# Two layers of a decoder on one core: in the first feed-forward, the last four tiles leave the transform earlier

## The chip, the cores and the metric

The kernel runs on one core of one Trainium2 chip. The metric is the device time of one execution in microseconds (us); the numbers of before are the median of three runs, and one further execution was taken with the hardware profiler. Five engines work side by side in a core: TensorE (PE in the profile, its weight loads PEld) multiplies matrices into PSUM, VectorE (DVE), ScalarE (ACT) and GpSimd (POOL) work elementwise, and SyncE (SP) here only issues transfers (DMAs).

## The reference, cut to what matters

The program is a decoder of two layers on `x` of 4 batches x 512 tokens x 512 features, each with self-attention, cross-attention and a feed-forward, every one followed by a residual sum and a layer norm. The change lies in the feed-forward of the first layer:

```python
gate = bitlinear(x, w_gate)                     # x in 8 bits per token, weights in {-1, 0, 1}
up = bitlinear(x, w_up)                         # both 512 -> 2048
intermediate = jax.nn.silu(gate) * up
return h_bitlinear(intermediate, w_down)        # act_quant(fwht(intermediate)) @ ternary(w_down).T
```

`fwht` is a Walsh-Hadamard transform over the 2048 features of a token. `act_quant` needs the largest value of a token after the transform, so nothing behind the transform can start for a token before all its 2048 features are there.

## The kernel before, in words

**Phases and lanes.** The six sublayers are phases A to F (C is the feed-forward of the first layer, D the self-attention of the second), and each phase is done for the batches 0 to 3: `ORDER` lists A0 ... F3. Each such task is a Python generator that emits some work and yields. `lanes` keeps two tasks alive and lets each emit one step in turn; I call one such turn a round. A new task starts when fewer than two are alive and the youngest one has yielded "next". So C1 runs beside C0, and is 16 rounds behind it; C2 starts in the round after C0 ends, C3 16 rounds behind C2, and D0 when C2 ends. Beside the lanes some weight preparation is advanced by one step per round (`BESIDE`): while C3 and D0 run, it loads and splits the weights of D.

**What sets the order.** The order of emission is a priority, not the final order: the tile framework places every instruction on its engine's queue by its own estimate of when operands and buffers are ready, and takes the earlier emitted one of those that are ready. On the chip each engine then works through its queue in order.

**Delays inside a task.** `Pipe.later(n, fn)` puts a piece of work on a list, and `tick()`, called at the start of each step, runs what has come due after `n` steps; `drain()` makes steps until the list is empty.

**Phase C of one batch (`l0_ffn`).** The 2048 features are 16 tiles of 128, tokens along the free axis (512). A step `o` of the loop at L734 multiplies gate and up of one tile (`pg` L740 and `pu` L742, 4 matmuls each, bf16). One step later `gate` multiplies by the token's scale (DVE, L709) and applies silu (ACT, L710). Two steps after that, `up` multiplies by the up part (DVE, L714) and splits the product into a rounded part `hh` (ACT, L716) and a rest `hl` (POOL, L717). Two steps later `had` multiplies both by the 128 x 128 Hadamard matrix (`ph`, two matmuls, L722 and L723: the transform's two passes). One step later `keep` copies `ph` from PSUM to `hw` (ACT, L728), and two steps after the copy SP stores `hw` to a scratch array in DRAM (L731). So tile 15, multiplied in step 15, is transformed in step 20, copied in step 21 and stored in step 23, and `drain` makes 8 steps after the loop.

The other half of the transform mixes the 16 tiles with one another. For that the scratch array is read back as 16 tiles `z` of 128 tokens' rows (SP, L253; the call stands behind the drain), with the 2048 features of a token rearranged; because every `z` tile holds rows from all 16 stores, the loads wait for the landing of the last store. Two more steps pass, and then 16 steps `had2` (L808, four matmuls in groups recorded as eight on the page) finish the transform. Behind each four of these come the largest value per token (DVE, L754), a copy (`q2f`, ACT, L756), the quantization (ACT L774, DVE L775), transposes (`q2T`, PE L781, copied by ACT at L786), and the down projection `dn` (16 matmuls, PE, L794).

Tiles of one kind share buffers: `g`, `hh`, `hl`, `hw` and others of a task take turns in 13 slots (`T_BUFS`), larger-lived ones such as `z`, `q2f` and the weights in 69 (`O_BUFS`), and all PSUM tiles in 8 banks.

Of the kernel before, what the change touches and what calls it, by code (L numbers as in the profile page):

```python
# [23 lines left out]
NT = 4  # L24
# [44 lines left out]
class Net:  # L69
# [590 lines left out]
    def l0_ffn(self, b):  # L660
        nc = self.nc
        pipe = Pipe()
# [50 lines left out]
        def up(o, pu, g):  # L713
            nc.vector.tensor_tensor(g, pu, g, ALU.mult)  # L714
            hi, lo = self.t("hh", F32R), self.t("hl", F32R)
            nc.scalar.copy(hi, g)  # L716
            nc.gpsimd.tensor_tensor(lo, g, hi.bitcast(F32), ALU.subtract)  # L717
            pipe.later(2, had, o, hi, lo)

        def had(o, hi, lo):  # L720
            ph = self.pb("ph")
            nc.tensor.matmul(ph, self.had, hi, start=True, stop=False)  # L722
            nc.tensor.matmul(ph, self.had, lo, start=False, stop=True)  # L723
            pipe.later(1, keep, o, ph)

        def keep(o, ph):
            w = self.t("hw")
            nc.scalar.copy(w, ph)  # L728

            to = scratch[:, o * P : (o + 1) * P, :].rearrange("i p t -> p i t")  # L730
            pipe.later(2, lambda: nc.sync.dma_start(to, w.rearrange("p (i t) -> p i t", i=NT)))  # L731

        tern = self.tern
        for o in range(16):  # L734
# [688 lines left out]
```

## Time and profile before

| | |
|---|---|
| time before, median of 3 runs | 1580.09 us (1579.72 to 1582.03) |
| the profiled execution's own time | 1580.57 us |
| its span, first to last instruction | 1578.9 us (1.67 us lie around it) |
| mean granted TensorE clock in it | 0.994 |
| PE busy in the span | 1512.4 us (96%) |
| DVE, ACT, POOL busy | 1214.0 us, 1041.7 us, 687.8 us |
| phase C, first gate matmul of C0 to last `dn` of C3 | 456 us to 759 us |

Durations further on come from the one profiled execution, and times of day are us from the start of its span. In the waits view a row names who waited for whom, with the total, how often, and the longest. In the timeline a row has the start, the length from the first to the last of a group, the engine, the line, the operation, the tiles (out<-in), the count, and in brackets how long the engine was idle before it and what ended that. In the table by stretches an engine's busy time is followed by its number of instructions, and PEclk is the share of the full clock that the throttle granted to TensorE.

### The profile page before, as it was taken

How to read it: one execution, taken by the hardware profiler on the slowest of the kernel's cores; microseconds unless marked ns; L12 is line 12 of the kernel's file. 1: busy time of each engine (PE TensorE's matmuls, PEld its weight loads, DVE VectorE, ACT ScalarE, POOL GpSimd, SP SyncE). 2: the span in 40 equal slices, each digit the busy share in tenths (PEclk: the TensorE clock that was granted, in tenths of full speed). 3: DMA queues.
4: the chain of work that ended last, by engine and by line, in shares of the span. 5: the costliest groups of instructions: out<-in, count | busy, mean ns of one | idle time of the engine just before them, and what ended most of it. 6: DMA issues, size and time to landing. Idle time of an engine off the chain costs nothing.

```text
span 1578.9 us, 25669 instructions
## 1 busy us (share of the span) xinstructions
PE 1512.4 (96%) x8222; PEld 1090.9 (69%) x8222; DVE 1214.0 (77%) x2594; ACT 1041.7 (66%) x2240; POOL 687.8 (44%) x704
## 2 busy tenths in 40 slices
PE   8999998999999999999999999999999999999996
PEld 6888775555544764477777668777687677787885
DVE  6486688898876678777577797767886898888896
ACT  5334667888778877887696864969634445545554
POOL 6665783656535303430435323353324344344342
PEclk9999999999999999999999999999999999999998
DMA  7044874444224534753434345633336630020101
GB/s 256 29 160 140 266 235 151 156 165 139 71 74 126 189 132 131 208 180 130 134 101 120 103 140 148 173 96 91 130 119 220 233 113 12 20 81 1 54 1 54
DMA packets 138759, 200.72 MB, mean 127 GB/s; under 512 B 17776, under 2 KB 52592, under 8 KB 138624
## 3 DMA queue, kind: packets, MB, share of 16 engines
q1 hardware_dynamic: 127584, 178.03, 35.5%
q10 hardware_dynamic: 6912, 12.59, 2.8%
q0 software_dynamic: 4128, 8.46, 2.2%
q8 instruction: 65, 1.06, 0.3%
q14 instruction: 70, 0.57, 0.1%
HBM read 121.94 MB, written 51.90 MB: 110 GB/s over the span
## 4 chain that ended last, share of the span: by engine, by line
PE 50%; DVE 11%; ACT 9%; issue 6%; DMA 3%; POOL 2%; SPq 0%; ACTq 0%; DVEq 0%; POOLq 0%
PE fg L1238 7%; PE facc L1221 5%; DVE fg L1194 3%; PE dT L986 3%; PE dn L794 2%; PE bo L500 2%; PE pg L740 2%; ACT de L976 2%; PE pu L742 2%; PE do L1006 2%; PE bT L249 2%; PE had L808 2%; PE bs L528 2%; PE ds L961 2%; PE dq L155 1%
## 5 line engine op out<-in xcount | busy, mean ns | idle before, releaser
L1194 DVE SCALAR_TENSOR_TENSOR fg<-fg,gs,fg 128x512 f32<-128x512 f32 x220 | 163.1, 745 | 30.4 <-ACT fg L1186 15.6
L976 ACT ACTIVATE de<-de,dm 128x128 f32<-128x128 f32 (+3 forms) x256 | 142.8, 562 | 11.5 <-DVE dm L972 11.3
L1238 PE MATMUL fg<-fxh,gu 128*128 128x512 f32 x352 | 140.4, 399 | 6.2 <-DVE fg L1194 3.1
L972 DVE CUSTOM_DVE_ANT_0 de<-ds,negm,thr 128x128 f32<-128x128 f32 (+3 forms) x256 | 126.3, 546 | 18.4 <-PE ds L961 15.8
L1238 PE MATMUL fg<-fxl,gu 128*128 128x512 f32 x352 | 137.5, 391 | 0.1
L717 POOL TENSOR_TENSOR hl<-g,hh 128x512 fp32r<-128x512 f32 x64 | 83.2, 1307 | 110.8 <-ACT hh L716 90.7
L484 POOL TENSOR_SCALAR be<-be,bsm 128x512 f32<-128x512 f32 x128 | 93.4, 742 | 85.3 <-DVE bsm L482 53.7
L1198 POOL TENSOR_TENSOR fg<-fg,fg 128x512 f32<-128x512 f32 x44 | 60.1, 1367 | 140.3 <-DVE fg L1194 56.7
L478 ACT ACTIVATE be<-bs,bsm 128x512 f32<-128x512 f32 x128 | 87.3, 689 | 32.4 <-DVE bsm L476 31.0
L898 POOL TENSOR_TENSOR dql<-dqf,dqh 128x512 fp32r<-128x512 f32 x32 | 41.4, 1295 | 150.6 <-ACT dqh L897 150.5
L986 PE MATMUL dT<-ident,de 128*128 128x128 f32 x640 | 91.3, 278 | 8.4 <-ACT de L976 6.4
L986 PEld LDWEIGHTS dT<-ident,de 128*128 128x128 f32 x640 | 71.7, 141 | 27.5 <-ACT de L976 14.8
L1238 PEld LDWEIGHTS fg<-fxh,gu 128*128 128x128 f32 x352 | 66.0, 188 | 30.6 <-DVE fg L1194 13.5
L476 DVE TENSOR_REDUCE bsm<-bs 128x1 f32<-128x512 f32 x128 | 83.0, 674 | 2.3 <-PE bs L528 2.3
L249 PEld LDWEIGHTS bT<-ident,be 128*128 128x128 f32 x512 | 54.9, 141 | 29.5 <-issue 15.6
L1238 PEld LDWEIGHTS fg<-fxl,gu 128*128 128x128 f32 x352 | 66.2, 188 | 12.8 <-DVE fxl L147 0.4
L1186 ACT ACTIVATE fg<-fg,gs 128x512 f32<-128x512 f32 x88 | 60.1, 683 | 20.6 <-PE fg L1238 20.6
L249 PE MATMUL bT<-ident,be 128*128 128x128 f32 x512 | 71.2, 280 | 1.4 <-POOL be L484 0.9
L500 PE MATMUL bo<-bpT,cT 128*64 128x512 f32 x256 | 71.4, 618 | 1.0 <-ACT bpT L491 1.0
L1212 POOL TENSOR_TENSOR fhl<-fg,fhh 128x512 fp32r<-128x512 f32 x44 | 58.5, 1330 | 29.9 <-ACT fhh L1211 29.7
L740 PE MATMUL pg<-qT,tb 128*128 128x512 bf16 x256 | 66.8, 381 | 4.4 <-ACT qT L702 2.8
L1190 ACT ACTIVATE fg<-fg,gs 128x512 f32<-128x512 f32 x44 | 30.3, 689 | 60.5 <-PE fg L1238 60.4
(357 smaller groups left out, 4685.3 us busy)
## 6 DMA issues: line engine op xcount, KB each, us to landing
x<-x SPq DMA_DIRECT2D x176, 256.0 KB, 3.2
had_scratch<-hw SPq DMA_DIRECT2D x64, 256.0 KB, 2.3
z<-had_scratch SPq DMA_DIRECT2D x64, 256.0 KB, 5.9
stk<-dqh SPq DMA_DIRECT2D x192, 64.0 KB, 2.1
tw<-in_wd_t SPq DMA_DIRECT2D x32, 256.0 KB, 4.0
p<-in_gu_p SPq DMA_DIRECT2D x22, 256.0 KB, 3.1
gu_codes<-gu SPq DMA_DIRECT2D x22, 256.0 KB, 3.1
gu<-gu_codes SPq DMA_DIRECT2D x22, 256.0 KB, 4.6
```

The lines of the kernel that those rows point to most:

```text
L249: self.nc.tensor.transpose(pt[:, i * P : (i + 1) * P], srcs[i][:, j * P : (j + 1) * P], self.ident)
L476: nc.vector.tensor_reduce(sm[:, h : h + 1], ps, AX.X, ALU.max, negate=True)
L478: nc.scalar.activation(e, ps, AF.Exp, bias=sm[:, h : h + 1], accum_out=sm[:, 2 + h : 3 + h])
L484: nc.gpsimd.tensor_scalar(es[h][i], es[h][i], sm[:, 4 + h : 5 + h], 1.0, ALU.mult, ALU.mult)
L500: nc.tensor.matmul(po[0][h * 64 : h * 64 + 64, :], cT[j][:, c : c + 64], pTs[h], start=j == 0, stop=j == NT - 1)
L717: nc.gpsimd.tensor_tensor(lo, g, hi.bitcast(F32), ALU.subtract)
L740: nc.tensor.matmul(pg, tern["wg_t"][k, c][:, m], qT[k], start=k == 0, stop=k == NT - 1)
L972: nc.vector.tensor_tensor_reduce(es[i], ps, self.negm[:, 384 - P * i :], -1.0, self.thr[:, i : i + 1], ALU.add, ALU.min, n4[:, i : i + 1])
L976: nc.scalar.activation(es[i], es[i], AF.Exp, bias=n4[:, i : i + 1], scale=-1.0, accum_out=den[:, hh * 4 + i : hh * 4 + i + 1])
L986: nc.tensor.transpose(pt[:, o + (i - j) * P : o + (i - j + 1) * P], es[i][:, j * P : (j + 1) * P], self.ident)
L1194: self.emitted["DVE"] = nc.vector.scalar_tensor_tensor(y[u], ps, s, y[u], ALU.mult, ALU.add)
L1238: nc.tensor.matmul(ps, self.gu[i, u][:, g * P : (g + 1) * P], xT[g][n], start=n == 0, stop=n == 1)
```

## The change

For the tiles `o` of 12 and over, `had` calls `keep` at once where it had put it off by one step, and `keep` puts the store off by one step where it had been two. For the tiles under 12 nothing changes. No instruction is added or removed; the last tile's store is emitted two steps earlier, so that the drain behind the loop of gate tiles has 6 steps where it had 8, in each of the four batches.

```diff
             nc.tensor.matmul(ph, self.had, lo, start=False, stop=True)
-            pipe.later(1, keep, o, ph)
+
+            if o < 12:
+                pipe.later(1, keep, o, ph)
+            else:
+                keep(o, ph)
 
         def keep(o, ph):
             w = self.t("hw")
             nc.scalar.copy(w, ph)
 
             to = scratch[:, o * P : (o + 1) * P, :].rearrange("i p t -> p i t")
-            pipe.later(2, lambda: nc.sync.dma_start(to, w.rearrange("p (i t) -> p i t", i=NT)))
+            pipe.later(2 if o < 12 else 1, lambda: nc.sync.dma_start(to, w.rearrange("p (i t) -> p i t", i=NT)))
```

## The prediction

> **What bounds the kernel now.** I read the page first: whom the time belongs to.
>
> ```profile
> PE 1512.4 (96%) x8222; PEld 1090.9 (69%) x8222; DVE 1214.0 (77%) x2594; ACT 1041.7 (66%) x2240; POOL 687.8 (44%) x704
> ...
> PE 50%; DVE 11%; ACT 9%; issue 6%; DMA 3%; POOL 2%; SPq 0%; ACTq 0%; DVEq 0%; POOLq 0%
> ```
>
> TensorE is busy in 96% of the span. The change adds no PE work and takes none away, so all it can move is PE's idle time, 66.5 us in the whole span, and the clock at which PE runs. Next, the waits of PE in the stretch of phase C (440 to 770 us):
>
> ```profile
> PE had L808 <- DMA z<-had_scratch: 3.4, 2, 2.4
> PE pg L740 <- ACT qT L702: 2.8, 2, 1.9
> ...
> ```
>
> The first row is the one that the change aims at: twice, 3.4 us in all, the second half of the transform waits for `z`, which waits for the last store. It can only be at the ends of C1 and C3: behind C0 and C2 the gate matmuls of the next batch fill PE. I look at the end of C1, PE first (two answers of the timeline):
>
> ```profile
> 543.12 0.48 PE L722 MATMUL ph<-hh,had 128*128 128x512 f32 x1
> 543.44 0.40 PE L723 MATMUL ph<-hl,had 128*128 128x512 f32 x1
> ...
> 555.14 1.13 PE L808 MATMUL had<-had,z 128*128 128x128 f32 x8 [2.38 <-DMA z<-had_scratch]
> ```
>
> The last tile's passes end at 543.84, and PE stands for 2.38 us until 555.14. What lies between is on ACT and SP:
>
> ```profile
> 543.37 1.09 ACT L786 COPY q2T<-q2T 128x1024 bf16<-128x1024 bf16 x1
> 544.27 1.40 ACT L774 ACTIVATE q2f<-q2f,am 128x512 f32<-128x512 f32 x2
> 545.51 0.64 ACT L756 COPY q2f<-had 128x512 f32<-128x512 f32 x1
> 545.97 0.66 ACT L728 COPY hw<-ph 128x512 f32<-128x512 f32 x1
> 546.45 1.42 ACT L774 ACTIVATE q2f<-q2f,am 128x512 f32<-128x512 f32 x2
> 547.69 0.65 ACT L756 COPY q2f<-had 128x512 f32<-128x512 f32 x1
> 548.15 0.68 ACT L728 COPY hw<-ph 128x512 f32<-128x512 f32 x1
> ...
> ```
>
> ```profile
> 548.85 0.36 SPq L731 DMA_DIRECT2D had_scratch<-hw  x1
> 551.24 1.76 SPq L253 DMA_DIRECT2D z<-had_scratch  x4
> ```
>
> The copy of tile 15 could have started at 543.84 and starts at 548.15: 4.31 us behind work of C0 that stands ahead of it in ACT's queue (tile 14: 3.49 us). SP doesn't hold anything up: the store goes out at the end of the copy, lands 2.27 us later, the first `z` goes out 0.12 us after that and takes 3.76 us. Last, what the standstill does to the clock, in the table by stretches (PEclk is the third figure from the right):
>
> ```profile
> 494.00:498.00 4.00, 2.14 (x11) 0.98 (x9) 2.41 (x4) 3.23 (x6) 1.35 (x2) 1.00 0.23 66
> 552.70:555.10 2.40, 0.05 (x1) 0.00 (x0) 2.40 (x6) 1.96 (x3) 0.00 (x0) 1.00 0.94 265
> 556.40:559.80 3.40, 3.40 (x10) 1.20 (x9) 1.36 (x3) 2.71 (x5) 0.00 (x0) 0.50 0.97 299
> 559.80:563.00 3.20, 3.20 (x31) 2.36 (x30) 1.44 (x3) 1.01 (x1) 0.00 (x0) 1.00 1.04 386
> ```
>
> From 556.4 to 559.8 the granted clock is half. The down projection of those us takes 5.30 us for its 16 matmuls, where those of 565.81 and 574.34 take 3.62: 1.68 us more. So this one wait costs 2.38 + 1.68 = 4.06 us.
>
> **The change part by part.** *The copy at once (16 copies: four tiles, four batches).* ACT does the same copies, 0.57 to 0.70 us each, only ahead of a round's other work. At the end of C1 the copy of tile 15 finds ACT in the `q2T` copy that ends at 544.46, and tile 14's may come between, until 545.1. It thus starts 0 to 1.3 us after its passes; I take 0.6 and a gain of 3.7 us (bounds 3.0 and 4.3). At the end of C3 the passes end at 698.61 and the copy starts at 701.56, 2.95 us late; with the same 0.6 the gain is 2.3. Should a copy reach the head of ACT's queue before its passes are done, ACT waits in order, with silu, the `hh` casts and `q2f` queued behind it, and POOL, DVE and then PE behind those. The row nearest to that is ACT waiting for `ph` before `hw`: 1.1 us in two waits over the 64 copies. Sixteen such waits of 0.4 to 0.6 us would be 6 to 9 us of ACT, which is idle for 2 to 6 us in every 20 us of the gate steps, so in part on the path; nearest is that row of 1.1 us, in which no wait of PE lies. I take 0.
>
> *The store after one step.* SP's queue carries the same 64 stores of 0.36 us each. They pass no transfer of this batch, since `z` needs all of them. In C2 they and `z` are moved past the last loads of D's weights (SP issues those from 640 to 654 us, between the stores); the weights are needed at 672 us by the `bo` matmuls, and SP issues one in 0.46 us, so a delay of one or two of them is hidden. I take 0; uncovered it would be the 0.4 us of the wait that the `bo` matmuls show. The `hw` buffers come free a step sooner; ACT waits for buffers of this pool in hardly any place (0.7 us for a landing store), worth -0.7 to 0, taken as 0.
>
> *The drain, two steps shorter.* This moves more than it seems. All of C0 behind its drain is emitted two rounds earlier against C1's gate steps, C1's own end two rounds earlier as well, and C2 starts two rounds sooner; C2 and C3 repeat it, and from D0 on all is as it was, four rounds sooner. Three places count.
>
> (a) End of C1. Chain before, from the end of the passes to `had2`: 555.14 - 543.84 = 11.30 us; PE's cover, work of C0, lasted until 552.75, 8.91 us. The chain falls by 3.7 to 7.6 us. The cover changes too: there are two rounds of C0 less in it. Two `had2` groups (2 x 0.9) and the first down projection (3.45) now come before C1's last passes, 5.3 us; the second down projection (3.45) and its neighbours' transposes (two, 0.9 in all) come into reach, 4.4 us, if ACT has delivered them. ACT is full here, 18.88 of the 20 us from 530 to 550, but only 13.95 of the 20 before, where two rounds of C0 now move, so I think it will. Cover 8.0 us, chain 7.6: the wait closes, narrowly. Gain 2.38, and with it the slow clock, 1.68.
>
> (b) End of C3: chain 708.50 - 698.61 = 9.89, wait 0.97, cover 8.92. After: chain 7.6, cover 8.0. Gain 0.97.
>
> (c) C0 and C2: `had2` comes two gate steps earlier. In C0 it started at 517.24; a gate step is 2.2 us, so it would stand at 512.8. The first `z` landed at 512.67, and this can't be earlier, as C0's last copy followed its passes at once (504.63 to 504.67). That just fits. Cost 0 to 2.2 us (one gate step), taken as 0.3, near the row. In C2, 668.37 less two steps of 2.45 is 663.5; `z` went out at 661.41 and landed at 665.99, but its copy was 3.2 us late, which goes. Cost 0 to 2.5 us, taken as 0.2.
>
> Sum against the profiled execution: 2.38 + 1.68 + 0.97 - 0.5 = 4.5 us off its own time of 1580.57 (span 1578.9 and 1.67 around it), 1576.1. The median of the runs stands 0.48 lower, so that I predict 1575.6. What is late next is ACT's `q2T` copy before a down projection (1.4 us of PE's waits now).
>
> The row says that a wait of 2.38 us was followed by half clock, while the 1.86 us from 494.46 and the 0.97 us from 707.53 were not. [...]
>
> **The rivals.** *The cover goes with the chain (slower).* Place: the ends of C1 and C3. If the second down projection isn't ready there, the cover is 8.91 - 5.3 = 3.6 us in both against a chain of 7.6: two waits of 4.0 us. Each is followed by a slow stretch of 1.7 us. Together 11.4 against 5.0 now, 6.4 us more: about 1586.5. It decides from the point at which the two waits with their clocks exceed 5.0 us, that is from some 1 to 2 us of wait in each place. For it: that projection's last operand came at 554.17, 10 us behind the passes. Against it: ACT has room in the rounds before.
>
> *A draw.* Chain and cover shrink alike; C1's wait stays near 2 us with its slow clock, C3's goes: 1579. For it: both are a matter of two rounds.
>
> *It doesn't do what it says.* The copies' priority rises by one round only; ACT's queue is arranged by estimated readiness, and a copy that the estimate takes to be ready late stays behind C0's work; then the chain and the wait remain: 1580. For it: tile 14's copy, due a round earlier than tile 15's, was as late. Against it: in C0 copies do start 0.04 us after the passes.
>
> **How the numbers follow.** The forecast gets 0.50, with a range of its own of 1573.5 to 1576.9; slower 0.23; the draw 0.15; nothing 0.12. About 0.2% or 3.2 us is what a measurement of this kernel can tell from no change. So faster 0.50, same 0.27, slower 0.23. The range goes from 1573.0 (all of the 5.0 us, and 2 us of small waits behind) up to 1584.5, which takes in the draw, nothing, and the lighter half of the slower rival.
>
> **What would show it.** Right: PE's wait for `z` under 1 us in all; tile 15's copies at the ends of C1 and C3 within 1.3 us of their passes; no half clock between 540 and 720 us; the last `dn` of C3, at 759 us before, some 4 us sooner, and the rest of the program shifted by that. Wrong: a wait for `z` of 2 us or more, at whichever batch; a second slow stretch; or a gain in phase C that is given back in phase D or F, where PE's queue would then be in another order.

## The result, and the profile after

The changed kernel is slower: 1591.57 us, the median of four runs (1586.68 to 1593.28), against 1580.95 us (1579.72 to 1582.03) for the kernel before. The ratio is 1.0065, with a 95% interval of 1.0043 to 1.0087. The same kernel run once more on another chip, against the kernel before on that chip, gave 1.0081 (1.0067 to 1.0094).

The page of the changed kernel, the rows that answer to those shown of before:

```profile
PE 1517.7 (95%) x8222; PEld 1092.4 (69%) x8222; DVE 1215.9 (76%) x2594; ACT 1041.8 (65%) x2240; POOL 687.8 (43%) x704
PE 47%; DVE 13%; ACT 9%; issue 6%; DMA 4%; POOL 2%; SPq 0%; ACTq 0%; DVEq 0%; POOLq 0%
```

The profiled execution is the slowest of the four (1593.28 us). Its span is 1591.6 us against 1578.9 before, 12.7 more. PE has as many instructions as before, but is busy for 5.3 us more (1517.7 against 1512.4) and idle for 7.4 us more (73.9 against 66.5). So there are two things to find: new waits, and the same matmuls at a lower clock. The waits of PE in phase C (440 to 790 us), who waited for whom, total, how often, longest:

```profile
PE had L812 <- DMA z<-had_scratch: 4.6, 1, 4.6
PE had L812 <- DVE q L779: 3.4, 1, 3.4
PE pg L744 <- ACT qT L702: 2.8, 2, 1.9
...
PE ph L723 <- POOL hl L717: 1.2, 2, 0.9
...
PE had L812 <- ACT hw L732: 0.7, 1, 0.7
```

The wait for `z` that the change aimed at is there in both places and longer: 3.42 us at the end of C1 (2.38 before) and 4.57 us at the end of C3 (0.97 before). The second row names DVE, but this is the same wait: the first `z` landed at 557.88 us and DVE's `q` ended within 0.01 us of it. The last two rows have no like before: 1.2 us for `hl` (0.88 in C1 and 0.36 in C3), and 0.7 us for `hw` at a `had2` of C2. Here is the end of C1 on PE:

```profile
545.57 0.50 PE L723 MATMUL ph<-hl,had 128*128 128x512 f32 x1 [0.88 <-POOL hl L717]
545.91 3.63 PE L798 MATMUL dn<-tb,q2T 128*128 128x512 bf16 x16
...
551.00 0.40 PE L723 MATMUL ph<-hl,had 128*128 128x512 f32 x1
551.24 0.62 PE L785 MATMUL q2T<-ident,q 128*128 128x128 bf16 x8
551.70 2.90 PE L812 MATMUL had<-had,z 128*128 128x128 f32 x24
558.02 1.13 PE L812 MATMUL had<-had,z 128*128 128x128 f32 x8 [3.42 <-DVE q L779]
558.98 5.30 PE L798 MATMUL dn<-tb,q2T 128*128 128x512 bf16 x16
```

The last tile's passes end at 551.40, 7.56 us later than before, because C0's first down projection (545.91) and one more `had2` group now run ahead of them. Only 3.20 us of C0's work lie behind the passes (until 554.60), where there were 8.91. Then PE stands until C1's first `had2`, and the down projection behind that takes 5.30 us where the one ahead took 3.63: the clock again. ACT and SP in the same stretch (timeline):

```profile
543.49 0.65 ACT L716 CAST hh<-g 128x512 fp32r<-128x512 f32 x1
545.44 0.68 ACT L716 CAST hh<-g 128x512 fp32r<-128x512 f32 x1
551.56 0.57 ACT L732 COPY hw<-ph 128x512 f32<-128x512 f32 x1
552.50 1.03 ACT L790 COPY q2T<-q2T 128x1024 bf16<-128x1024 bf16 x1
```

```profile
552.16 0.36 SPq L735 DMA_DIRECT2D had_scratch<-hw  x1
554.54 1.75 SPq L253 DMA_DIRECT2D z<-had_scratch  x4
```

The change does what it says: the copy starts 0.16 us behind the passes (4.31 before), the store goes out at once, and the chain from the passes to `had2` falls from 11.30 to 6.62 us. The first two rows show another side of it. The `hh` casts of the tiles 14 and 15 come at 543.49 and 545.44, where they came at 537.01 and 539.56: C0's quantization, moved two rounds earlier, and copies of earlier tiles stand ahead of them on ACT. Which of the two makes PE wait for `hl`, the first two experiments tell.

The clock, in the table by stretches (PEclk is the third figure from the right):

```profile
554.60:558.00 3.40, 0.00 (x0) 0.01 (x1) 2.26 (x8) 1.48 (x4) 0.28 (x1) 1.00 0.65 178
559.10:562.40 3.30, 3.30 (x10) 1.15 (x8) 0.69 (x1) 0.58 (x1) 0.00 (x0) 0.50 0.95 289
716.10:722.80 6.70, 5.45 (x17) 3.17 (x18) 1.12 (x2) 1.66 (x4) 0.00 (x0) 0.50 0.94 289
1142.80:1146.10 3.30, 3.30 (x8) 1.31 (x9) 1.88 (x5) 1.47 (x5) 1.75 (x3) 0.50 0.59 222
```

Half clock follows both waits. The stretch at 559 had its like before (556.4). New are the one behind the wait of C3, 6.83 us long, in which PE was busy for 5.45 us (its `dn` matmuls there start 427 ns apart, against 216 ns at the full clock, so that I put the loss at half of this, 2.7 us), and one at 1142.7 (1.7 us lost). These two make 4.4 of the 5.3 us of additional busy time; the other 0.9 us I can't put to a place. That the stretch at 1142.7 is the change's doing isn't shown: the second profile of the changed kernel has none there but one at 938.2, and the faster kernel of the first experiment has one at 927.4. Of the 7.4 us of additional idle time 7.0 lie in phase C.

By stage, PE is 0.6 us late at the first gate matmul of C0 already (458.56 us against 457.97; the 456 us in the table of before is the start of the transposes ahead of it), 2.9 us at the start of C2 (behind the end of C1), 3.8 us at C2's last gate steps, and 11.6 us at the end of C3. This stays so through phase D, and the stretch at 1142.7 adds most of the rest. So phase C carries 11.0 us of the 12.7, and no later stage gave more than 1 us back.

### The profile page after: what moved, and what is told of

Same layout as the page of the kernel before. It is cut to its first block, busy times and chain, and to the rows that moved or that the text cites. A ratio compares the mean times of both kernels' runs of the same rounds, so it can differ in the third digit from the quotient of the medians.

```text
span 1591.6 us, 25678 instructions
## 1 busy us (share of the span) xinstructions
PE 1517.7 (95%) x8222; PEld 1092.4 (69%) x8222; DVE 1215.9 (76%) x2594; ACT 1041.8 (65%) x2240; POOL 687.8 (43%) x704
## 4 chain that ended last, share of the span: by engine, by line
PE 47%; DVE 13%; ACT 9%; issue 6%; DMA 4%; POOL 2%; SPq 0%; ACTq 0%; DVEq 0%; POOLq 0%
PE fg L1242 7%; PE facc L1225 5%; PE dT L990 3%; PE dn L798 3%; DVE fg L1198 3%; ACT de L980 2%; PE bo L500 2%; PE had L812 2%; PE do L1010 2%; PE bT L249 2%; PE pu L746 2%; PE pg L744 2%; PE ds L965 1%; PE dq L155 1%; PE bs L528 1%
## 5 line engine op out<-in xcount | busy, mean ns | idle before, releaser
L812 PE MATMUL had<-had,z 128*128 128x128 f32 x512 | 67.2, 281 | 8.7 <-DMA z<-had_scratch 4.6
L1190 ACT ACTIVATE fg<-fg,gs 128x512 f32<-128x512 f32 x88 | 60.1, 683 | 20.8 <-PE fg L1242 20.6
L812 PEld LDWEIGHTS had<-had,z 128*128 128x128 f32 x512 | 63.0, 194 | 12.2 <-DVE q L779 8.3
```

Of the source, the lines that this page charges most:

```text
L812: nc.tensor.matmul(ps[:, c * P : (c + 1) * P], z[i * 4 + g][:, c * P : (c + 1) * P], self.had16, start=True, stop=True)
```

## The experiments

Each kernel was timed against the kernel before on its own chip; there the kernel before had medians from 1577.35 to 1578.22 us, so ratios are compared, not times. The first two experiments are to tell two theories apart: that the waits come from the lost cover (C0's rounds shifted against C1's), or from the copies and stores in their new places.

**The changed kernel with its two rounds given back**, ahead of the loads of `z`:

```diff
         yield from pipe.drain()
 
+        yield
+        yield
         z = [self.load(self.o("z"), ...
```

> The changed kernel with two empty steps put back between the drain and the z loads, so that only the early copy and store are left of the change and the lanes stand to each other as before. Theory (the shorter drain took PE's cover away at the ends of C1 and C3): PE's queue there is that of before, 8.9 us of C0's (C2's) work between the last passes and the first second-transform group, and the chain falls from 11.3 and 9.9 us to some 7 to 8; no wait for z at either place, no half clock there, so 1580.9 less 3 to 5 us: 1576 to 1578. Rival (the copies at once and the early stores disturb ACT's and SP's queues): it stays slow, 1588 to 1593.

Measured: 1575.62 us, ratio 0.9989 (0.9979 to 0.9998). PE's order is that of before again, and the wait for `z` is nearly gone:

```profile
PE had L814 <- DMA z<-had_scratch: 0.6, 1, 0.6
```

The early copies and stores alone lose nothing on balance. The gain over the kernel before is 1.7 us on the medians, less than the theory's 3 to 5. The trace shows why in part (rows of PE and ACT at the end of C1, then of PE at the end of C3):

```profile
542.87 0.45 PE L723 MATMUL ph<-hl,had 128*128 128x512 f32 x1
545.74 0.67 ACT L732 COPY hw<-ph 128x512 f32<-128x512 f32 x1
...
692.10 0.50 PE L723 MATMUL ph<-hl,had 128*128 128x512 f32 x1 [0.85 <-POOL hl L717]
694.08 0.50 PE L723 MATMUL ph<-hl,had 128*128 128x512 f32 x1 [0.36 <-POOL hl L717]
```

The last passes of C1 end at 543.33 here, near their old time, and the copy of tile 15 starts 2.41 us behind them, not 0.16 us; the first `z` lands 8.55 us behind the passes, 0.2 us before C1's first `had2`, so that the wait closes narrowly. And PE waits 1.2 us for `hl`, as long as in the changed kernel, though no round is shifted.

**The kernel before with the drain alone shorter**; copies and stores as before:

```diff
         ln = self.ln_tile()
-        yield
-        yield
```

> The kernel before, with copies and stores as they were, but without the two steps between the z loads and the second transform, so that C0's work behind its drain is two rounds earlier against C1's gates, as in the changed kernel. Theory: the cover falls to some 3 to 4 us as in the changed kernel while the chain isn't shortened, so waits for z of 6 to 8 us at the ends of C1 and C3 with a slow clock behind each: slower than the changed kernel or like it, 1591 to 1600. Rival (copies and stores are to blame): as before, 1579 to 1583.

Measured: 1595.66 us, ratio 1.0116 (1.0103 to 1.0129). PE at the ends of C1 and C3 (rows of the timeline):

```profile
549.06 0.40 PE L723 MATMUL ph<-hl,had 128*128 128x512 f32 x1
...
558.78 2.05 PE L806 MATMUL had<-had,z 128*128 128x128 f32 x8 [6.13 <-DMA z<-had_scratch]
...
720.88 2.05 PE L806 MATMUL had<-had,z 128*128 128x128 f32 x8 [4.67 <-DMA z<-had_scratch]
```

The passes end at 549.46, the cover is 3.19 us, the same as in the changed kernel, and without the shorter chain the wait is 6.13 us. So the two rounds cause the loss, and the early copies and stores win part of it back. That refutes the rival. PE waits for no `hl` here, so that this wait comes from the early copies and not from the two rounds alone: all profiles that have it have the copies at once. A third wait for `z` is at C2's `had2`, 2.53 us, where the first experiment had 0.6 and the changed kernel none.

**The order on PE.** In the instruction order of both kernels, C1's first `had2` group stands ahead of C0's second down projection. If that order is what takes the cover away, one more step ahead of `had2` in C1 and C3, which puts the down projection first, closes the wait in either kernel:

```diff
         yield
         yield
+        if b % 2:
+            yield
         q2T = {}
```

In the kernel before:

> The kernel before with one more empty step ahead of the second transform in C1 and C3 alone; in PE's queue the second down projection of C0 (C2) then stands ahead of the first second-transform group of C1 (C3), where before it stood behind it. Theory with the queue's order as the reason of the waits: 3.45 us more cover against unchanged chains of 11.3 and 9.9 us, so no wait for z at the end of C1 (2.4 before) nor of C3 (1.0), no half clock there: 1580.9 less 3 to 5, 1576 to 1578. Rival (the down projection isn't ready in time, ACT is what is short): PE waits for ACT's q2T copy instead, 1579 to 1583.

Measured: 1580.03 us, ratio 1.0018 (1.0009 to 1.0027). The timeline of PE at the end of C1 has no gap now:

```profile
542.34 3.62 PE L796 MATMUL dn<-tb,q2T 128*128 128x512 bf16 x16
...
550.37 3.72 PE L796 MATMUL dn<-tb,q2T 128*128 128x512 bf16 x16
```

The second down projection starts at 550.37 instead of 556.10. But the kernel didn't get faster. Its waits of PE in phase C:

```profile
PE pg L740 <- ACT qT L702: 4.9, 3, 2.2
PE dn L796 <- ACT q2T L788: 2.2, 2, 1.7
PE had L810 <- DMA z<-had_scratch: 1.2, 1, 1.2
```

One of C1's last down projections now waits 1.67 us for `q2T` (589 us), and C3's first gate matmul waits 2.15 us for `qT` (until 642.3) with half clock behind it until 645.7; C2's `had2` waits 1.2 us. The theory was right on the place and wrong on the total, which lies in the rival's range; the rival's wait for `q2T` is there too, but not where it was expected.

In the changed kernel:

> The changed kernel with the same one more step in C1 and C3. Theory: cover 3.2 plus 3.45 us against chains of 6.6 and 7.8 us, so waits for z of 0 to 1.2 us where the changed kernel has 3.4 and 4.5, and mostly no slow clock: 7 to 10 us off its 1591.6, 1581 to 1585. Rival (ACT is short, the down projection isn't ready): 1588 to 1593.

Measured: 1583.76 us, ratio 1.0041 (1.0026 to 1.0057): as expected. No wait for `z` is left at the end of C1 and 1.0 us at that of C3, and the same wait of 2.1 us for `qT` appears, with half clock from 642.8.

**The rounds given back at another place**: four steps instead of two behind the loads of `z` in the changed kernel, so that `z` goes out two rounds before it would with the first experiment's edit:

```diff
         ln = self.ln_tile()
         yield
         yield
+        yield
+        yield
```

> The changed kernel with two more empty steps behind the z loads instead of ahead of them: the loads are emitted as early as in the changed kernel, the second transform as late as in the kernel before. Theory (cover): PE's queue and the chain are those of the padded drain (e1), SP issues z when the last store has landed in both: the same time as e1 within 2 us, 0.997 to 1.001 of the kernel before, no wait for z at the ends of C1 and C3. Rival (z emitted early gets in the way of other transfers on SP): 1.005 or more.

Measured: 1574.92 us, ratio 0.9980 (0.9969 to 0.9991). PE waits for no `z` in phase C, and for no `hl`. This version is faster than both kernels, by 2.9 us on the medians against the kernel before.

**The two halves of the change.** Copy at once, store two steps later as before (the drain has 7 steps): only the `if o < 12` of `had` is kept.

> Half of the change: for the last four tiles the copy at once, but the store two steps behind it as before; the drain has 7 steps. In PE's queue the first down projection of C0 then still stands behind C1's last passes, as before the change, and only one second-transform group (0.9 us) has moved ahead of them: cover 8.0 us against a chain of 7 to 8. Theory (cover and chain, decided by where that projection stands): no wait for z or one under 1 us at the ends of C1 and C3, 0.997 to 1.001 of the kernel before. Rival (each step off the drain costs alike, half of the changed kernel's loss): 1.003.

Measured: 1581.74 us, ratio 1.0031 (1.0019 to 1.0042). Store one step after the copy, copy one step after the passes (7 steps as well): only the `2 if o < 12 else 1` of `keep` is kept.

> The other half: the copy one step behind the passes as before, the store one step behind the copy; the drain has 7 steps too. PE's queue is that of e6. Theory: cover 8.0 us, and a chain that is as long as before where the copy waits in ACT's queue (11.3 and 9.9 us): waits for z of about 3.3 and 1.9 us, mostly with a slow clock behind them, 1.001 to 1.004 of the kernel before, and slower than e6 by 3 us or more. Rival (the shorter drain alone counts, the copy's place doesn't): the same time as e6 within 1.5 us.

Measured: 1583.78 us, ratio 1.0041 (1.0027 to 1.0056), 2.0 us more than the copy's half: between the theory's 3 us or more and the rival's 1.5 or less. C1's first `had2` in the one and in the other (timeline of PE):

```profile
554.28 1.13 PE L811 MATMUL had<-had,z 128*128 128x128 f32 x8 [0.90 <-DMA z<-had_scratch]
```

```profile
554.39 1.13 PE L808 MATMUL had<-had,z 128*128 128x128 f32 x8 [2.72 <-DMA z<-had_scratch]
```

The waits at the ends are near the theory's: under 1 us in the first, and 2.72 and 1.26 us in the second, where it had about 3.3 and 1.9. The time of the first isn't, it is the rival's: its waits at the ends are under 1 us and no half clock lies in phase C, yet it is 3.9 us slower on the medians. PE is idle for 14.7 us from 440 to 780 us, where it was for 11.9 in the profile of before and 13.4 in a second one. The second is the one to compare with, since it lacks 31 matmul records as this one does, and a missing record counts as idle time. Against it I can place a wait of C2's `had2` for `z` (1.26 us) and three waits for `hl` (1.2 us), less 0.9 us that the waits at the ends of C1 and C3 are shorter. The rest of the 3.9 us stays open.

**The copy's half with its round given back**: that kernel and one `yield` ahead of the loads of `z`.

> The copy-only half (e6) with one empty step put back ahead of the z loads, so that the lanes stand to each other as before and only the place of the 16 copies is changed. Theory (the shift of the lanes costs, the copies don't): 0.997 to 1.000 of the kernel before, some 0.3 to 0.5% under e6. Rival (e6's 1.0031 came from the copies' new place in ACT's queue): 1.002 to 1.004, like e6.

Measured: 1575.53 us, ratio 0.9989 (0.9979 to 1.0000). The copies in their new place cost no more than they win (PE waits 1.2 us for `hl` here too); the loss of the half is that of its one round.

**One round less and nothing else**: the kernel before without one of its two steps behind the loads of `z`.

> The kernel before with one of the two empty steps behind the z loads taken out: half of e3's shift, copies and stores as before. PE's queue at the end of C1 is that of e6 and e7, the first down projection of C0 still behind C1's last passes. Theory: cover 8.0 us against chains of 11.3 and 9.9: waits for z of about 3 and 2 us, like e7, 1.003 to 1.005, less than half of e3's 1.0116, since the down projection hasn't changed its place. Rival (every step costs the same): 1.0055 to 1.0065.

Measured: 1587.73 us, ratio 1.0070 (1.0055 to 1.0085), above the theory and nearer to the rival. At the end of C1:

```profile
556.89 2.04 PE L807 MATMUL had<-had,z 128*128 128x128 f32 x8 [4.22 <-DMA z<-had_scratch]
```

The cover was 8.04 us, as expected of one round. The chain was what I had wrong: the copy started 4.9 us behind the passes (4.31 before), which makes it 12.26 us. Half clock for 6.83 us followed here, and 3.41 us at C3.

**Does it repeat?** The changed kernel, unaltered, on another chip:

> The changed kernel, unaltered, timed again beside the kernel before on one chip, since its ratio rests on four runs. Theory: the waits for z at the ends of C1 and C3 are there again, 3 to 4.5 us each, the last passes of C1 again some 5 to 8 us later than in the kernel before, and the ratio lies within 1.005 to 1.009; with e3 at 1.0116 and e1 at 0.9989 the early copies and stores are then worth some 0.3 to 0.6% inside the shortened drain. Rival (a good part of the 1.0065 was the slow clock of single executions): 1.003 or less.

Measured: 1589.89 us, ratio 1.0081 (1.0067 to 1.0094). Its waits for `z` are 3.16 us at C1, with no half clock behind it, and 3.31 us at C3, with half clock. A further profile of the kernel before:

> The kernel before, unaltered, one more profile, to see which of its own numbers belong to the execution and which to the kernel. Theory: the wait for z at the end of C1 is there again (1.5 to 2.5 us) and about 1 us at the end of C3; whether the clock halves behind the first depends on where the wait falls in the windows in which the clock is set (the starts of half clock within each trace lie whole multiples of 3.413 us apart), so it may be missing, and the time is then 1.7 us shorter. Rival: the half clock stands behind that wait in every execution.

Measured: 1579.98 us in that one execution. The wait at C1 is 2.25 us, and half clock follows at 556.7; at C3 it is 0.49 us. So these two profiles agree with the rival as well; it is the two of the changed kernel that differ, with half clock behind the wait at C1 in one of them only.

The experiments in one table. All times are us in the profiled execution: the chain from the end of the last passes to the first `had2`, the cover that PE has behind those passes, and the wait, first for C1 and then for C3.

| kernel | steps less | chain / cover / wait, C1 | chain / cover / wait, C3 | ratio |
|---|---|---|---|---|
| before | 0 | 11.30 / 8.91 / 2.38 | 9.89 / 8.92 / 0.97 | 1 |
| copy only | 1 | 8.93 / 8.04 / 0.90 | 8.96 / 8.04 / 0.92 | 1.0031 |
| store only | 1 | 10.76 / 8.04 / 2.72 | 9.30 / 8.04 / 1.26 | 1.0041 |
| one step less | 1 | 12.26 / 8.04 / 4.22 | 11.29 / 8.05 / 3.24 | 1.0070 |
| changed | 2 | 6.62 / 3.20 / 3.42 | 7.76 / 3.19 / 4.57 | 1.0065 |
| two steps less | 2 | 9.32 / 3.19 / 6.13 | 7.86 / 3.19 / 4.67 | 1.0116 |

The cover depends only on how many rounds C0 is shifted, not on what shortened the drain. One round costs 0.9 us, a `had2` group that goes in front. The second costs 4.85 us: the first down projection (3.45), a group's transposes and one more `had2` group go in front of the last passes, and nothing follows at the other end. The times don't follow the cover alone: the first round taken out of the kernel before cost 0.70%, the second some 0.46% more.

**What stays open.** Where the rest of the loss lies in the kernels that are one round shorter, and why the down projection put first gives its gain back at C1's last down projections and C3's first gate step, is seen only as waits for `qT`, `q2T` and C2's `z`; no experiment separates them. A version that keeps C0's work early and puts the last passes ahead of the first down projection wasn't tried.

## Why the prediction was wrong

**The copy, the store (right in the changed kernel, with luck).** I put the copy 0.6 us behind its passes; it came 0.16 us behind at both ends. But that was behind passes that themselves came 7.56 us later at C1. In the setting that I had in mind, with the passes near their old time, the copies came 2.41 and 2.42 us behind them (the first experiment), still behind C0's work on ACT, and the gain of 3.7 us at C1 would have been 1.9. The store followed, and SP held nothing up. The chain was predicted at 7.6 us and was 6.62 and 7.76; the difference between the two lies in the landing of the store, 2.26 us after its issue at C1 and 3.54 at C3. The copies were not free, though. I had written that casts queue behind a copy on ACT and that POOL and PE then wait, and had taken it as 0; PE's waits for `hl` came to 1.2 us in both profiles of the changed kernel and in that of the first experiment. It is less than the copies win: the ratio with the rounds given back was 0.9989.

**The cover (the step that failed).** Part (a) took 5.3 us out of the cover and put 4.4 back: "the second down projection ... come into reach, ... if ACT has delivered them", and so "Cover 8.0 us"; part (b) took the same 8.0 for C3. It was 3.20 and 3.19. The 5.3 us went as worked out (8.91 - 3.20 = 5.7), the 4.4 never came. ACT had delivered: the `q2T` copy for that projection ended at 553.53 us, and the projection ran at 558.98. It stood behind C1's `had2` in PE's queue, and PE took the two in that order (558.02, then 558.98), so it waited for a `z` that it doesn't need. The trace of before shows the same order (ACT, then PE):

```profile
553.15 1.02 ACT L786 COPY q2T<-q2T 128x1024 bf16<-128x1024 bf16 x1
...
555.14 1.13 PE L808 MATMUL had<-had,z 128*128 128x128 f32 x8 [2.38 <-DMA z<-had_scratch]
556.10 5.30 PE L794 MATMUL dn<-tb,q2T 128*128 128x512 bf16 x16
```

The operand was there at 554.17, and PE stood idle until 555.14 with a ready down projection in its queue. I had this row, and used 554.17 only as a sign that ACT was late. It could have told me that readiness doesn't decide here. The order comes from the emission: the round in which C0 yields "next" runs no `tick`, so that C0's second down projection falls due a round after C1's first `had2` has been emitted. Moving C0 by whole rounds doesn't change this, since C1's end moves with it. The experiment with one more step ahead of `had2` shows it from the other side: there the projection ran at 550.37 and the wait was gone.

**The slower rival (its mechanism came true).** It put the cover at 3.6 us in both places, with two waits of 4.0 us, each followed by a slow stretch. Measured were 3.2 us, and waits of 3.42 and 4.57. Its condition was wrong in the same way as my forecast: it asked for a projection that "isn't ready", and this one was ready but queued. Its price of 6.4 us was too low as well: 10.6 us on the medians and 11.7 on the other chip. Three terms were missing in the profiled execution: the slow stretch of C3 lasted 6.83 us instead of the 3.41 that I had seen once; PE waited 1.2 us for `hl`, the cost of the early copies; and a further stretch of half clock fell at 1142.7, 1.7 us, which may be chance.

**The small costs (c).** I took 0.5 us for C0 and C2, for waits for `z`. In the changed kernel neither waits for `z`, and the 0.6 us by which C0 is late were there before it began. A later `had2` of C2 waits 0.72 us for `hw`: the size was right by luck.

**The clock.** I read the half clock at 556.4 as the wait's doing. That held: all seven profiled executions with a wait for `z` of 2.2 us or more at the ends of C1 or C3 had half clock behind at least one of these waits, and the six without one had none there. But the same wait of the changed kernel at C1 had it in one profile (3.42 us) and not in the other (3.16 us).

**The draw and "it doesn't do what it says"** are refuted: the wait at C1 stays but C3's grows, and the copies did start at once.

## What to carry to other kernels

Count the cover of a wait from the order in the engine's own queue, not from what is ready: PE stood here until 558.02 us at a `had2` that waited for `z`, with a down projection behind it whose operand had been there since 553.53, and the trace shows this as an operand that lands before its user starts while something else is waited for. A step taken out of one task's drain moves everything behind it against the other tasks, so look at what then goes in front of the chain that was to be shortened. If only the chain is to be shorter, keep the offset between the tasks: with the two rounds given back behind the loads of `z`, the same edit was worth 0.2% (0.9980, 0.9969 to 0.9991).

## What the runs showed of the hardware

**Where the half clock began.** In the profile of the changed kernel the stretches of half clock between 200 and 1560 us begin at 245.03, 559.06, 716.07 and 1142.74 us: counted from the first, 0, 92, 138 and 263 times 3.4133 us. In that of the kernel before they begin at 245.74 and 556.36 us, 91 times as much apart. Those at 559.06, 1142.74 and 556.36 last 3.41 us, the other three 6.83.

**PE's idle time ahead of it.** I divided these two profiles from 200 to 1560 us into stretches of 3.4133 us, counted from the same starts, and added up PE's idle time in each stretch that began at the full clock, 787 in all. Five have 2.19 to 3.29 us, and half clock begins at the end of each. One with 1.86 us (the changed kernel's wait for `qT` from 495.05) has none behind it, one with 1.50 us (1139.33 to 1142.74) has, and the other 780, with 1.43 us at most, have none. The 1.50 us are three gaps ahead of `dT`, of 0.64, 0.16 and 0.70 us, so here it was not one long gap. The changed kernel's wait of 3.42 us at C1 fell as 1.05 and 2.37 us into two stretches, with half clock behind the second; the 3.16 us in its second run fell as 1.93 and 1.28 us, and the clock stayed.

**So the price of one and the same wait differed.** The changed kernel's wait at C1 had half clock behind it in one profile and not in the other. These numbers fit a price that depends on where a wait lies among the stretches; no experiment moved a wait and nothing else. Its four runs of 1593.28, 1592.67, 1590.47 and 1586.68 us had mean granted clocks of 0.991, 0.992, 0.993 and 0.995, in the same order; that the place of the waits is the reason for this order too isn't shown, since only one of them was profiled.
